# Matmuls of ones ahead of two score matmuls at the start of layer 1's cross-attention

## The chip, the core and the metric

The kernel runs on one core of one Trainium2 chip. A core has five engines with a queue each: TensorE (in the profile PE for the matmuls and PEld for the loading of their weights), VectorE (DVE), ScalarE (ACT), GpSimd (POOL) and SyncE (SP, which here only issues DMAs). Matmuls write to PSUM, which has eight banks of 2 KB per partition. The metric is the device time of one execution in microseconds, the median of several runs. The profile is of one execution, taken apart from these runs.

## The reference

A decoder of two layers works on x, 16 sequences of 256 tokens with 128 channels, and on a context of 16 x 64 rows. Everything is float32. Each layer adds a self-attention, a cross-attention and a feed-forward part with experts to x. The change lies where layer 1's self-attention ends and its cross-attention begins:

```python
def _L1_xattn_ref(x, latents, w_q, w_kv, w_out, b_out):   # 16 heads of 8 channels
    q = latents @ w_q.T                                   # latents: the normed x
    k, v = jnp.split(x @ w_kv.T, 2, axis=-1)              # x here: the context
    ...
    attn = jnp.einsum('blhd,bshd->bhls', q, k) * SCALE
    attn = jax.nn.softmax(attn, axis=-1)
    out = jnp.einsum('bhls,bshd->blhd', attn, v)
    return out.reshape(B, L, DIM) @ w_out.T + b_out

x = x + _L1_attn_ref(_layernorm(x), ...)
x = x + _L1_xattn_ref(ctx_1024, _layernorm(x), ...)   # the context and the latents
x = x + _L1_ffn_ref(_layernorm(x), ...)
```

(In the call as the kernel computes it, queries come from the normed x and keys and values from the context, so every token has 64 scores for each of 16 heads.)

## The kernel before, in words

The kernel works through the layers in phases. Layer 1's self-attention is one phase; cross-attention and the feed-forward part of layer 1 are the next one, and the last. Each phase opens pools of PSUM banks of its own on the banks that the phase before has given back. Self-attention has four banks of scores, three small ones (a pool of tag `m`, L1584) and one of outputs. The last phase has one tile `sx` of four banks, two small banks (again a tag `m`, in the pool `ps_m` of that phase) and two for the feed-forward part. `misc` (L1511) takes the next of the small banks.

Within the phase, x is cut into 8 chunks of 512 tokens, and a chunk into 4 row tiles of 128 tokens. A part is a small function that issues one step for one row tile, one pair of tiles (a sequence) or one chunk. The order of the parts is written out by hand: a word such as `S2:0` means part S2 for chunk 0, and every engine executes its own instructions in the order in which the words issue them. There is a list of words for the start, one plan that repeats for the chunks, and one list for the end. Self-attention's order is written out in the same way. Where the phases meet, an engine's instructions of the new phase can lie between the last ones of the old phase.

The parts for row tile i that matter here, in the order in which a tile goes through them:

- `S` (L1979, its matmul L1983) multiplies the keys of the tile's sequence with its queries: four float32 matmuls, one for each group of 32 partitions, into one half of `sx`. Tiles 0, 2, ... take the one half, tiles 1, 3, ... the other. A float32 matmul is two pieces in the profile.
- `G` (L1990, VectorE) finds the greatest score per head, negated; `B` (L1994, VectorE) subtracts it, reading `sx` for the last time and writing `px` in SBUF; `E` (L2002, ScalarE) is the exponential.
- `A` (L2008 and L2009, GpSimd) adds halves of the 64 probabilities; `R` (L2016 and L2017, VectorE) finishes the sum and takes the reciprocal; `Q` (L2022, GpSimd) spreads it.
- `T` with a half of the heads (`flip`, L2039, its matmul L2043) transposes four blocks of 128 x 128 probabilities into a small bank `tx`; `C` (L2052, ScalarE) copies that bank to SBUF as `pTx`.
- `V` (L2061) multiplies with the values, and so on to the output of the cross-attention.

The start of the phase is these words: S1 and S0, then G0, G1 and B0 on VectorE, S2 (which overwrites tile 0's half of `sx`, so it waits for B0), G2, E0, T01 (tile 0, second half of the heads), B1 and B2, E1, S3 (which in the trace starts when B2 has ended), C01 and so on. S0 and S1 of chunk 1 follow, whose maximum is `G0:1`.

The last steps of self-attention that matter here are the product `y` with the output weights (L1712, TensorE, into one of the three small banks) and its addition to x (L1716, VectorE).

At the very start of the whole kernel stand 18 matmuls of ones by ones (L1048), 36 pieces in the profile. The tile `ones` (L107) is 128 x 128 in SBUF and never changes.

Of the kernel before, what the change touches and what calls it, by code (L numbers as in the profile page):

```python
# [22 lines left out]
P = 128  # L23
# [5 lines left out]
TPC = CH // P  # L29
# [19 lines left out]
W = D + 2  # L49
# [18 lines left out]
def kernel(ctx: ExitStack, tc: tile.TileContext, a: dict, out: bass.AP):  # L68
    nc = tc.nc
# [37 lines left out]
    ones = const.tile([P, P], F32, tag="ones", name="ones")  # L107
# [140 lines left out]
    with ExitStack() as ph:  # L248
# [229 lines left out]
        PARTS = ((0, slice(0, P)), (1, slice(P, 3 * P)))  # L478
# [39 lines left out]
        def flip(u):  # L518
            b, pair = u
            halves = tp_of[u] = [  # L520
                ps_m.tile([P, 2, 3, HP], F32, tag="m", name=f"t0_{b}_{pair}_{r}") for r in range(2)
            ]
            for i in range(2):
                pr = pr_of.pop((b, 2 * pair + i))
                for blk in range(3):
                    for r in range(2):
                        rows = slice(r * HP, (r + 1) * HP)
                        nc.tensor.transpose(  # L528
                            halves[r][:, i, blk, :], pr[rows, blk * P : (blk + 1) * P],
                            ident[rows, rows],  # L530
                        )

        def flipped(u, r):
            b, pair = u
            if r == 0:
                pT_of[u] = pp.tile([P, 2, 3, 2, HP], F32, tag="pT", name=f"pT0_{b}_{pair}", bufs=3)
            nc.vector.tensor_copy(pT_of[u][:, :, :, r, :], tp_of[u][r])  # L537
# [500 lines left out]
        with tc.manual_schedule(engines=ordered | {mybir.EngineType.Pool}):  # L1038
# [104 lines left out]
            for i in range(steps // 2):  # L1143
# [4 lines left out]
                def unit(k, j, *rest):  # L1148
                    if not 0 <= j < n:
                        return  # L1150
                    u = units[j]
                    {
                        "S": scores, "T": flip, "V": values, "G": greatest, "E": exponentials,
                        "R": reciprocal, "N": scaled, "C": flipped, "O": values_out,
                    }[k](u, *rest)

                for tok, lag in plan_of:
                    k = tok[0]
# [157 lines left out]
    with ExitStack() as ph:  # L1316
# [87 lines left out]
        def down(i):  # L1404
            s = state[i]
            ps = s["y"] = ps_m.tile([P, D], F32, tag="m", name=f"y0_{i}")
            for f in range(NF0):
                nc.tensor.matmul(  # L1408
                    ps, s["hT"][:, f, :],
                    dn0[:, bass.ds(s["e"], 1), f, :].rearrange("p e d -> p (e d)"),  # L1410
                    start=(f == 0), stop=(f == NF0 - 1),
                )
# [96 lines left out]
    held = {}  # L1509

    def misc(key, shape):  # L1511
        held[key] = room["m"].tile(shape, F32, tag="m", name="_".join(map(str, key)))
        return held[key]
# [11 lines left out]
    def part_root(what, c):  # L1525
        mv = held["mv", what, c]
        ve = lnp.tile([P, TPC], F32, tag="ve", name=f"ve_{what}_{c}")
        nc.gpsimd.tensor_scalar(ve, mv[:, :, 1], LN_EPS, None, ALU.add)
        rstd = lnp.tile([P, TPC], F32, tag=f"rstd_{what}", name=f"rstd_{what}_{c}")
        nc.gpsimd.tensor_tensor(rstd, ve, nhalf, ALU.pow)  # L1530
        held["rstd", what, c] = rstd
        if what == "f":
            nb = held["nb", c] = lnp.tile([P, TPC], F32, tag="nb", name=f"nb_{c}")
            nc.gpsimd.tensor_tensor(nb, mv[:, :, 0], rstd, ALU.mult)
            nc.gpsimd.tensor_scalar(nb, nb, -1.0, None, ALU.mult)
# [429 lines left out]
    with ExitStack() as ph:  # L1965
# [69 lines left out]
        def shares_out(b):  # L2035
            held["rT", b] = xp.tile([P, N], F32, tag="rT", name=f"rT_{b}")
            nc.scalar.copy(held["rT", b], held.pop(("rt", b)))

        def flip(u, half):  # L2039
            ps = misc(("tx", u, half), [P, 4, P])  # L2040
            for m in range(4):
                h = 8 * half + 2 * m
                nc.tensor.transpose(  # L2043
                    ps[:, m, :],
                    held["pr", u][:, h : h + 2, :].rearrange("p h j -> p (h j)"), ident,
                )
# [178 lines left out]
        def added(c, t):  # L2225
            if ("yo", c) not in held:
                held["yo", c] = hbp.tile([P, TPC, D], F32, tag="yo", name=f"yo_{c}")
            yo = held["yo", c]
            nc.vector.tensor_tensor(
                yo[:, t, :], x[c][:, t, :],  # L2230
                bank(t) if c == NCHUNK - 1 else held.pop(("yf", c, t)), ALU.add,
            )
            held["made", c, t] = True
            if ("made", c, t ^ 1) in held:
                t -= t % 2
                r0 = c * CH + t * P
                nc.sync.dma_start(
                    out_rows[r0 : r0 + 2 * P, :].rearrange("(t p) d -> p t d", p=P),
                    yo[:, t : t + 2, :],
                )  # L2240

        PARTS = {"xt": xt, "xc": xc, "xb": xb, "xq": xq, "xQ": xQ, "xr": lambda c: part_root("x", c)}
# [10 lines left out]
        for i in range(TPC):  # L2253
            for key, what in (
                ("S", scores), ("G", greatest), ("B", below), ("E", exponential), ("R", sums),
                ("A", quarters), ("Q", shares_of),
            ):
                PARTS[f"{key}{i}"] = lambda c, i=i, what=what: what(TPC * c + i)
            for half in range(2):
                PARTS[f"T{i}{half}"] = lambda c, i=i, half=half: flip(TPC * c + i, half)  # L2260
                PARTS[f"C{i}{half}"] = lambda c, i=i, half=half: flipped(
                    TPC * c + i, half, nc.scalar.copy
                )
                PARTS[f"D{i}{half}"] = lambda c, i=i, half=half: flipped(
                    TPC * c + i, half, nc.vector.tensor_copy
                )
            PARTS[f"d{i}"] = lambda c, i=i: down(c, i)
            PARTS[f"z{i}"] = lambda c, i=i: added(c, i)
# [21 lines left out]
        plan = [part.split(":") for part in PLAN.split()]  # L2290
        with tc.manual_schedule(engines=ordered | {mybir.EngineType.Pool}):
            for word in (
                "xs1:2 S1:0 S0:0 G0:0 G1:0 B0:0 S2:0 G2:0 E0:0 T01:0 B1:0 B2:0 E1:0 S3:0"
                " C01:0 A1:0 E2:0 G3:0 T11:0 A0:0 T21:0 T10:0 B3:0 C11:0 R1:0 Q1:0 S0:1 S1:1"
                " C21:0 R0:0 T00:0 E3:0 T30:0 C10:0 G0:1 A2:0 T20:0 C00:0 C30:0 Q0:0 C20:0"
                " G1:1 A3:0 K0:2 P0:0 V0:0 B1:1 B0:1 R3:0 U0:0 T31:0 S2:1 E0:1 O0:0 Q3:0"
                " C31:0 xt:2 Y0:0 R2:0 G2:1 Q2:0 E1:1 X0:0 B2:1 xc:2 P1:0 U1:0 A0:1 E2:1"
            ).split():
                part, c = word.split(":")
                PARTS[part](int(c))  # L2300
            for c0 in range(1, 7):
                for part, lag in plan:
                    if 0 <= c0 - int(lag) < NCHUNK and (part, c0 - int(lag)) not in begun:
                        PARTS[part](c0 - int(lag))
            for word in (
                "xb:7 fs0:6 R0:7 V1:6 A1:7 O1:6 S3:7 a1:5 z1:4 A2:7 T21:7 m1:5 Y1:6 C21:7"
                " X1:6 fs1:6 h2:5 a2:5 T10:7 fr:6 m2:5 h3:5 C10:7 a3:5 T11:7 R1:7 C11:7 m3:5"
                " T01:7 C01:7 fn:6 G3:7 Q0:7 T00:7 T20:7 D20:7 k2:5 C00:7 Q1:7 h4:5 k3:5"
                " k1:5 pk:7 B3:7 a4:5 P0:7 ft:6 m4:5 U0:7 R2:7 j4:5 fc:6 V0:7 fl:6 O0:7 h0:6"
                " Y0:7 a0:6 d3:5 d0:5 E3:7 Q2:7 fg:6 fe:6 T30:7 A3:7 T31:7 C30:7 X0:7 m0:6"  # L2310
                " z3:5 z0:5 fs0:7 C31:7 fq:6 d2:5 fw:6 R3:7 h1:6 Q3:7 fW:6 a1:6 z2:5 P1:7"
                " U1:7 V1:7 O1:7 Y1:7 m1:6 X1:7 h2:6 a2:6 fs1:7 m2:6 h3:6 a3:6 m3:6 j3:6"
                " h4:6 fr:7 fn:7 ft:7 a4:6 m4:6 fc:7 d1:5 z1:5 fl:7 j2:6 k4:6 h0:7 k1:6 a0:7"
                " fg:7 d3:6 m0:7 fe:7 z3:6 d0:6 fq:7 h1:7 fw:7 a1:7 fW:7 m1:7 h2:7 i1:7 a2:7"
                " z0:6 d2:6 m2:7 h3:7 j1:7 a3:7 e0:7 d1:6 m3:7 j3:7 h4:7 e1:7 i2:7 z2:6 a4:7"
                " m4:7 j2:7 e3:7 z1:6 k4:7 e4:7 e2:7 z3:7 z2:7 z1:7 z0:7"
            ).split():
                part, c = word.split(":")
                PARTS[part](int(c))
# [59 lines left out]
```

## Time and profile before

| | us |
|---|---|
| median of three runs | 1401.31 (1401.13 to 1402.62) |
| the profiled execution | 1399.55 |
| its span, first to last instruction | 1397.8 |

| stretch of the span, us | PE busy | DVE busy | ACT busy | POOL busy | granted clock |
|---|---|---|---|---|---|
| 0 to 830 | 800.62 | 616.96 | 485.04 | 473.44 | 1.00 |
| 830 to 1149 (self-attention of layer 1) | 305.29 | 296.08 | 304.70 | 124.76 | 0.99 |
| 1149 to 1180 (where the phases meet) | 23.61 | 19.36 | 14.59 | 9.50 | 0.78 |
| 1180 to 1398 | 206.36 | 173.23 | 138.30 | 135.13 | 1.00 |

All times are microseconds from the first instruction. The page cuts the span into 40 equal slices and gives each engine's busy share as a digit in tenths, and in the line PEclk the granted clock of TensorE in tenths of full speed. The same can be asked for any stretch. In the timeline a row is the start, the time it took, the engine, the line, the operation, what it writes and reads, its shape and how many pieces are merged; in brackets stands how long the engine was idle before, and what released it. The chain that ended last is followed back from the last instruction: each step is what released the step after it, or what stood before it on its engine. A matmul's end is modelled, and the pieces of one row overlap.

### The profile page before, as it was taken

How to read it: one execution, taken by the hardware profiler on the slowest of the kernel's cores; microseconds unless marked ns; L12 is line 12 of the kernel's file. 1: busy time of each engine (PE TensorE's matmuls, PEld its weight loads, DVE VectorE, ACT ScalarE, POOL GpSimd, SP SyncE). 2: the span in 40 equal slices, each digit the busy share in tenths (PEclk: the TensorE clock that was granted, in tenths of full speed). 3: DMA queues.
4: the chain of work that ended last, by engine and by line, in shares of the span. 5: the costliest groups of instructions: out<-in, count | busy, mean ns of one | idle time of the engine just before them, and what ended most of it. 6: DMA issues, size and time to landing. Idle time of an engine off the chain costs nothing.

```text
span 1397.8 us, 38026 instructions
## 1 busy us (share of the span) xinstructions
PE 1335.9 (96%) x13209; PEld 997.3 (71%) x13209; DVE 1105.6 (79%) x4481; ACT 942.6 (67%) x2533; POOL 742.8 (53%) x1226
## 2 busy tenths in 40 slices
PE   9999999999999999799899989999999987899998
PEld 7777777777777777689899966666666654566665
DVE  5776877777777768677679769999999977988874
ACT  6776666767675766354233349999999984776663
POOL 6463748575666656745533373543344314667751
PEclk9999999999999999999999999999999998999999
DMA  6773000000000000467667520000000000113112
GB/s 163 235 241 90 2 5 10 10 7 11 7 10 9 17 9 19 152 201 239 198 225 233 172 71 24 17 15 12 17 2 3 3 2 1 31 43 73 39 43 65
DMA packets 80085, 95.33 MB, mean 68 GB/s; under 512 B 19564, under 2 KB 62828, under 8 KB 79896
## 3 DMA queue, kind: packets, MB, share of 16 engines
q1 hardware_dynamic: 65064, 45.72, 11.9%
q10 hardware_dynamic: 10512, 38.28, 8.1%
q0 software_dynamic: 4320, 8.92, 1.9%
q8 instruction: 106, 1.74, 0.5%
q14 instruction: 83, 0.68, 0.2%
HBM read 63.72 MB, written 29.16 MB: 66 GB/s over the span
## 4 chain that ended last, share of the span: by engine, by line
PE 67%; ACT 17%; DVE 12%; issue 2%; POOL 1%; another core or an unknown queue 1%; DMA 0%; ACTq 0%; DVEq 0%; POOLq 0%
ACT p L1752 8%; PE pqk L418 8%; PE o L550 5%; PE s L473 5%; PE y L450 4%; PE g L1390 4%; PE t L528 4%; PE u L1390 4%; PE y L1408 4%; PE pv L435 3%; PE t L1770 3%; PE g L2173 2%; ACT pT L1781 2%; PE s L1730 2%; PE o L1794 2%; PE u L2173 2%
## 5 line engine op out<-in xcount | busy, mean ns | idle before, releaser
L512 POOL TENSOR_SCALAR p<-p,rs 128x128 f32<-128x128 f32 (+1 forms) x512 | 213.3, 431 | 166.1 <-DVE rs L506 124.3
L498 ACT ACTIVATE p<-p,nm 128x128 f32<-128x128 f32 (+1 forms) x512 | 226.4, 446 | 24.5 <-DVE nm L486 20.1
L1752 ACT ACTIVATE p<-p,nm 128x256 f32<-128x256 f32 x512 | 220.9, 508 | 1.7 <-DVE nm L1741 0.4
L1741 DVE CUSTOM_DVE_ANT_0 p<-s,strip 128x256 f32<-128x256 f32 x512 | 186.7, 419 | 14.7 <-PE s L1730 13.8
L537 DVE COPY pT<-t 128x384 f32<-128x384 f32 x256 | 130.2, 550 | 38.9 <-PE t L528 37.5
L486 DVE CUSTOM_DVE_ANT_0 p<-s,strip 128x128 f32<-128x128 f32 (+1 forms) x512 | 154.2, 348 | 0.5 <-PE s L473 0.2
L1419 POOL DMA_INDIRECT rows_out<-yr,to x71 | 68.8, 969 | 116.3 <-DVE yr L1417 110.6
L1770 PEld LDWEIGHTS t<-ident,p 64*128 64x128 f32 x2048 | 79.7, 139 | 54.4 <-ACT pT L1781 15.3
L550 PEld LDWEIGHTS o<-pT,v 128*64 128x64 f32 x1024 | 64.2, 138 | 66.4 <-issue 34.1
L429 ACT ACTIVATE k<-pqk 128x512 f32<-128x512 f32 x64 | 38.1, 596 | 108.3 <-PE pqk L418 108.3
L1770 PE MATMUL t<-ident,p 64*128 64x64 f32 x2048 | 102.4, 231 | 8.1 <-ACT pT L1781 2.7
L1398 ACT ACTIVATE gs<-gs 128x512 f32<-128x512 f32 x71 | 44.7, 630 | 85.3 <-DVE gs L1397 73.5
L473 PE MATMUL s<-k,q 64*128 64x128 f32 (+1 forms) x1024 | 100.4, 332 | 0.3 <-DVE nm L486 0.3
L550 PE MATMUL o<-pT,v 128*64 128x256 f32 (+1 forms) x1024 | 99.0, 335 | 0.6 <-DVE pT L537 0.6
L498 ACT ACTIVATION_READ_ACCUMULATOR p<-p,nm 128x1 f32 x512 | 97.9, 191 | 0.0
L528 PE MATMUL t<-ident,p 64*128 64x64 f32 x1536 | 81.2, 228 | 14.2 <-ACT pre L742 4.7
L528 PEld LDWEIGHTS t<-ident,p 64*128 64x128 f32 x1536 | 68.3, 138 | 35.8 <-POOL p L512 9.0
L1730 PE MATMUL s<-k,q 32*128 32x256 f32 x1024 | 86.3, 409 | 1.4 <-DVE nm L1741 1.4
L1781 ACT COPY pT<-t 128x512 f32<-128x512 f32 x144 | 81.1, 588 | 5.1 <-PE t L1770 4.3
L444 DVE COPY v<-pv 128x512 f32<-128x512 f32 x64 | 44.2, 691 | 50.5 <-PE o L550 28.0
L1390 PE MATMUL g<-xTs,gu 128*128 128x128 f32 x568 | 76.9, 279 | 3.6 <-ACT xTs L1362 3.5
L1390 PE MATMUL u<-xTs,gu 128*128 128x128 f32 x568 | 76.8, 276 | 3.3 <-issue 3.3
(375 smaller groups left out, 3356.1 us busy)
## 6 DMA issues: line engine op xcount, KB each, us to landing
gu<-in_L_ffn_gate_up_w ACTq DMA_DIRECT2D x71, 512.0 KB
rows_in<-zero SPq DMA_DIRECT2D x131, 130.0 KB
spread<-wrows SPq DMA_DIRECT2D x14, 512.0 KB
xr<-rows_in SPq DMA_DIRECT2D x71, 65.0 KB
y<-rows_out SPq DMA_DIRECT2D x16, 256.0 KB
out_x<-yo SPq DMA_DIRECT2D x16, 128.0 KB
x<-in_x SPq DMA_DIRECT2D x7, 256.0 KB
rows_out<-yr,to POOLq DMA_INDIRECT x71
```

The costliest lines, as they stand in the source:

```text
L473: nc.tensor.matmul(ps_of[b, h][:, cols], q[rows, u2, iq], k[rows, u2, 0:nk], start=True, stop=True,)
L486: nc.vector.tensor_tensor_reduce(out=pr[:, cols], in0=ps[:, cols], in1=strip[:, h, P : 2 * P] if it == 0 else strip[:, h, :], scale=1.0, s ...
L498: nc.scalar.activation(pr[:, cols], pr[:, cols], AF.Exp, bias=nm[:, it : it + 1], scale=-1.0, accum_out=sm[:, it : it + 1],)
L512: nc.gpsimd.tensor_scalar(pr[:, cols], pr[:, cols], rs[:, it : it + 1], 1.0, ALU.mult, ALU.mult)
L528: nc.tensor.transpose(halves[r][:, i, blk, :], pr[rows, blk * P : (blk + 1) * P], ident[rows, rows],)
L537: nc.vector.tensor_copy(pT_of[u][:, :, :, r, :], tp_of[u][r])
L550: nc.tensor.matmul(po[rows, c0:N], v[:, jt, h % 8 * DH : (h % 8 + 1) * DH], pT[:, 0:N] if jt == 0 else pT[:, N:], start=(jt == 0), stop=(j ...
L1390: nc.tensor.matmul(ps[:, f, :], gu[:, lo + f * P : lo + (f + 1) * P], xT, start=True, stop=True,)
L1730: nc.tensor.matmul(ps_of[b, h][:, it, :], q[rows, it * P : (it + 1) * P], k[rows, s4, :], start=True, stop=True,)
L1741: nc.vector.tensor_tensor_reduce(out=pr[:, it, :], in0=ps[:, it, :], in1=strip1[:, h, (1 - it) * P : (1 - it) * P + N], scale=1.0, scalar= ...
L1752: nc.scalar.activation(pr[:, it, :], pr[:, it, :], AF.Exp, bias=nm[:, it : it + 1], scale=-1.0)
L1770: nc.tensor.transpose(halves[r][:, k, jt, it, :], pr[rows, it, jt * P : (jt + 1) * P], ident[rows, rows],)
```

## The change

A new part `W` with a row tile and a half takes the small bank that the same tile's `T` will write, and issues 14 matmuls of `ones` by `ones` into its four quarters in turn, each starting and ending its own sum. `T` then uses the bank that `W` took, if there is one, and its transposes overwrite what the ones left. Two words are added to the list of the start: `W01:0` between B0 and S2 (the bank of T01), and `W11:0` between E1 and S3 (the bank of T11). On TensorE they stand directly ahead of the third and the fourth tile's scores. Nothing else is changed, and no result depends on the added products.

```diff
+        def keep(u, half, times):
+
+            ps = misc(("tx", u, half), [P, 4, P])
+            for k in range(times):
+                nc.tensor.matmul(ps[:, k % 4, :], ones, ones, start=True, stop=True)
+
         def flip(u, half):
-            ps = misc(("tx", u, half), [P, 4, P])
+            ps = held.get(("tx", u, half)) or misc(("tx", u, half), [P, 4, P])
...
             for half in range(2):
+                PARTS[f"W{i}{half}"] = lambda c, i=i, half=half: keep(TPC * c + i, half, 14)
...
-                "xs1:2 S1:0 S0:0 G0:0 G1:0 B0:0 S2:0 G2:0 E0:0 T01:0 B1:0 B2:0 E1:0 S3:0"
+                "xs1:2 S1:0 S0:0 G0:0 G1:0 B0:0 W01:0 S2:0 G2:0 E0:0 T01:0 B1:0 B2:0 E1:0 W11:0 S3:0"
                 " C01:0 A1:0 E2:0 G3:0 T11:0 A0:0 T21:0 T10:0 B3:0 C11:0 R1:0 Q1:0 S0:1 S1:1"
```

## The prediction

> **What bounds the kernel now.** I read the page's slices first. TensorE is busy nearly everywhere, and of the slices ahead of the last two, the one around 1170 us is the emptiest in the kernel and the only one whose granted clock shows less than 9.
>
> ```profile
> span 1397.8 us, 38026 instructions
> PE   9999999999999999799899989999999987899998
> PEclk9999999999999999999999999999999998999999
> ```
>
> One slice is 34.9 us; the 8 is the 34th, 1153 to 1188 us. There layer 1's self-attention ends and its cross-attention begins, and the change sits in it. Next I read that stretch in the timeline of TensorE (start, length, line, what it writes, count, idle time before and its releaser):
>
> ```profile
> 1159.32 0.71 PE L1712 MATMUL y<-wo,oT 128*128 128x128 f32 x4
> 1163.30 1.24 PE L1983 MATMUL sx<-kb,qx 32*128 32x256 f32 x8 [3.27 <-DVE px L1994]
> 1164.57 1.11 PE L2043 MATMUL tx<-ident,px 128*128 128x128 f32 x4
> 1168.15 1.24 PE L1983 MATMUL sx<-kb,qx 32*128 32x256 f32 x8 [2.47 <-DVE px L1994]
> 1169.32 2.91 PE L2043 MATMUL tx<-ident,px 128*128 128x128 f32 x12
> 1172.16 2.09 PE L1983 MATMUL sx<-kb,qx 32*128 32x256 f32 x16
> ```
>
> TensorE ends self-attention's last product y at 1160.03 and idles 3.27 us until S2, the third tile's scores, may overwrite the first tile's half of sx; before S3 it idles 2.47 us again. VectorE is the releaser both times. The third view is busy time per stretch; the columns are length, then PE, PEld, DVE, ACT, POOL, then the granted clock.
>
> ```profile
> 1157.34:1160.75 3.41, 2.69 (x12) 1.38 (x10) 1.62 (x4) 0.37 (x1) 0.00 (x0) 1.00 0.03 5
> 1160.75:1164.16 3.41, 0.86 (x8) 0.52 (x8) 2.50 (x3) 0.80 (x1) 0.00 (x0) 0.50 0.00 0
> 1164.16:1167.58 3.42, 1.50 (x8) 0.71 (x4) 2.97 (x3) 0.93 (x2) 0.00 (x0) 0.50 0.00 0
> 1167.58:1170.99 3.41, 2.84 (x16) 2.08 (x16) 2.02 (x3) 2.61 (x4) 2.69 (x3) 0.50 0.00 0
> 1170.99:1174.40 3.41, 3.41 (x23) 2.17 (x22) 2.15 (x6) 2.27 (x4) 2.98 (x5) 0.50 0.00 0
> ```
>
> The clock is half from 1160.75 to 1174.40, exactly four steps of 3.41 us. The other falls (566.83, 699.95, 843.31) last one step each, and all lie on the same 3.413-us grid. So this execution decides the clock at fixed moments, by what the step just ended held. S2 and S3 take 1.24 us here and 0.71 us at 1184.64, where the clock is full.
>
> The fourth view is the chain that ended last.
>
> ```profile
> 1168.15 1.24 PE sx L1983 x8
> 1169.39 2.84 PE tx L2043 x12
> 1172.23 2.06 PE sx L1983 x16
> 1174.29 0.02 issue
> 1174.31 2.37 DVE nmx L1990 x2
> ```
>
> It runs through TensorE at half speed to 1174.29, where the fifth tile's scores release VectorE. After that VectorE leads (9.3 of 10 us busy from 1180 to 1190), then TensorE (119.1 of 120 from 1220 to 1340), so what 1174.31 gains or loses should reach the end. I call that moment **G0:1**. At full clock those pieces, with S2 and the transposes before, would take about half: (1.28 + 0.9 + 1.24 + 2.84 + 2.06)/2 = 4.2 us. That is the most there is to win.
>
> **The change, part by part.** W01 stands behind S0 and y, ahead of S2. W11 stands behind the second tile's exponential and the first tile's transposes (T01), ahead of S3. Each is 14 products of ones, 128x128x128 in float32. L1048 shows the price: 18 products are 36 pieces, so 14 are 28. Read one by one in the timeline, its pieces start 0.213 us apart until 7.03 and 0.112 us apart afterwards (the clock record begins at 7.04). So 28 pieces cost 28 x 0.112 = 3.1 us at full clock and 6.0 us at half. Nothing is removed and no DMA is added; SP and POOL's queues are not passed.
>
> *When W01 may start.* Its bank is the first of a pool that opens where self-attention's pools close, so I take it that the first write waits for the last reader of all of self-attention's small banks. That is L1716, which adds y to x, behind the first maximum on VectorE:
>
> ```profile
> 1160.57 0.41 DVE L1716 TENSOR_TENSOR x<-x,y 128x256 f32<-128x256 f32 x1
> 1160.90 1.22 DVE L1990 TENSOR_REDUCE nmx<-sx 128x16 f32<-128x1024 f32 x1
> 1162.03 1.22 DVE L1994 TENSOR_TENSOR px<-sx,nmx 128x1024 f32<-128x1024 f32 x1
> ```
>
> 0.04 us of signal after 1160.98 gives 1161.02. Before the change nobody saw this wait: the first writer of these banks stood behind S2, which waits for the later L1994. Behind W01 on TensorE stand S2 and everything else; VectorE waits for S2 in G2 and then for nothing until S3.
>
> *Whether the clock is up.* For every grid step I summed the pieces' streaming time, weighted by the share of the array's rows and columns they use. The five steps ahead of a fall hold 0.4 to 1.13 us; every other step at full clock holds 1.26 or more. The step to 1160.75 holds 0.89, and W01 at 1161.02 adds nothing to it, so **the clock falls as before**. In steps at half clock the clock stayed down at 2.47 or less and rose at 2.86 or more. W01 fills 1164.16 - 1161.02 = 3.14 us of the next one, so I let it rise at 1164.16, ten us earlier than now.
>
> [...] Here the record falls 0.72 us after the last piece. [...]
>
> *Sum.* W01 runs 14.7 pieces by 1164.16; the other 13.3 take 1.5 us, to 1165.65. S2, ready at 1163.27, starts there and ends 0.7 later: G2 moves from 1164.61 to 1166.35, **+1.74**. The two subtractions behind it, B1 and B2 (1.14 us each), move as much; B2 ends at 1169.85. W11 starts after T01 (about 1166.8) and ends at 1169.9, under G2, B1 and B2: it costs nothing, and would cost what exceeds 3.1 us if that cover were shorter. S3 then takes 0.7 for 1.24, so G3 is 1.2 late. The 12 transposes and 16 score pieces in front of G0:1 need 1.3 + 1.07 us at full clock, and end near 1173.5. They are no longer last. **What is late next** is POOL: its half sums (L2008, L2009) start at 1168.22 behind the second exponential, which sits behind B1, and take 2.05 + 2.1 us for two tiles; moved by 1.74 they end at 1174.1. VectorE reads them (0.41 and 0.25 us, L2016, L2017) ahead of G0:1: 1174.75 for 1174.31, **+0.45**, say +0.5. The profiled execution would go from 1399.55 (span 1397.8 and 1.75 around it) to 1400.05. The three timed runs' median, 1401.31, lies 1.76 above that execution; the same half us gives **1401.8**.
>
> Another execution may have its grid elsewhere. Worked through with the same weights for all positions, the forecast's kind of fall (somewhere between 1158.9 and 1161.5) gives +0.4 to +2.1, since before the change too the clock comes back earlier at some of them.
>
> **Rivals.**
> - **A, the clock holds.** For: W01 shortens the idle time to 1.0 us, and for grid positions with boundaries from 1161.6 on it is already in the deciding step. Then W01 ends at 1164.15, G2 is 0.24 late, POOL's sums end at 1172.6, G0:1 comes at 1173.3: **-1.0** (1400.3), -0.2 where the old clock recovered sooner. Against: the profiled step of 0.89.
> - **B, W01's bank is free at once.** Its own bank was last read by L1693, which ends at 1157.7. W01 then starts at 1160.03, puts 0.72 us into the deciding step (1.61, no fall), ends at 1163.16 and hides wholly: G2 at 1164.0 (-0.6), POOL's sums 1171.75, G0:1 at 1172.4: **-1.9** (1399.4). Against: the pool's boundary.
> - **C, slower: the ones do not bring the clock back in time.** Place: W01 ahead of S2. If 3.14 of 3.41 us is not enough, all 28 pieces run at half: S2 starts at 1167.0, G2 at 1168.2 (+3.55), G0:1 by POOL at 1176.6: **+2.3** (1403.6). Should the clock still be down when W11 runs, S3 waits 6.0 us for it and comes at 1175.1 for 1168.15: +7 (1408). It decides from a rise later than 1167.6. For: 2.84 busy us did not suffice at 1170.99. Against: L1048 itself rises after its first filled step.
> - **D, the whole cold stretch is repaid** and POOL is not late: -4.2 (1397.1). Against: W01 alone is longer than the 2.28 us between 1161.02 and S2.
>
> **How the numbers follow.** Forecast 0.45, A 0.25, B 0.08, C 0.15 (a third of it the +7), D 0.07. Over 0.2%, 2.8 us and about what a measurement of this kernel can tell from no change, lie D on one side, and on the other the +7 and about half of the rest of C and the ends of the forecast: faster 0.07, within 0.81, slower 0.12. The range takes in A, B and the lesser C with a few tenths for the spread of the runs (1401.13 to 1402.62), 1399.2 to 1403.8; D, the +7 and some of C, 0.17, stay out.
>
> **What would show it.** Right: W01's first piece starts within 0.1 us of the end of L1716; the clock is half for one step only; its pieces change from 0.213 to 0.112 apart on the way; S2 starts near 1165.6, S3 near 1169.9 without idle time caused by W11; the fifth tile's maximum waits for L2017 and no longer for sx. Wrong: W01 next to y (B), clock 1.00 throughout (A), S2 at 1167 (C), or a later step that now falls because work has shifted against the grid: the step 1198.29 to 1201.71 holds only 1.28, and one more fall would cost up to 1.7.

## The result, and the profile after

| | before | after |
|---|---|---|
| median over the runs compared, us | 1400.91 (18 runs) | 1403.58 (18 runs) |
| ratio, 95% interval | | 1.0021 [1.0013, 1.003] |
| the profiled execution, us | 1399.55 | 1405.24 |

The change costs 0.21%, 2.9 us (1.8 to 4.2 by the interval). The forecast was 0.5 us. The page of the changed kernel, where code lines behind the insertion stand 6 lower than before:

```profile
span 1403.5 us, 38138 instructions
PE   9999999999999999799899989999999988899998
PEclk9999999999999999999999999999999999999999
```

The 112 added instructions are 56 matmul pieces and 56 weight loads. The 8 has become a 9 in PEclk: the cold stretch is gone from the page, and yet the kernel is slower.

Two executions of one kernel can't be laid over each other from their starts, because the part ahead of the change differs from one to the next: the last y (L1712) starts between 1156.97 and 1166.29 us in the executions below. So I cut each trace at two events. **Lead** is the stretch from the start of that y to the start of the ninth maximum on VectorE (L1990). **Rest** is the stretch from there to the end of the span; some expectations call it the tail. Before: lead 31.59, rest 206.93. After: lead 32.32, rest 208.78. So the change loses **0.73 us in the lead** and **1.85 us in the rest**, 2.58 together, within the interval of the runs.

**The lead.** The timeline of TensorE after the change (start, length, line, what it writes, count, idle before and its releaser):

```profile
1162.40 0.71 PE L1712 MATMUL y<-wo,oT 128*128 128x128 f32 x4
1164.12 4.93 PE L2043 MATMUL tx<-ones 128*128 128x128 f32 x28 [1.00 <-DVE x L1716]
1168.98 0.71 PE L1983 MATMUL sx<-kb,qx 32*128 32x256 f32 x8
...
1170.12 3.29 PE L2043 MATMUL tx<-ones 128*128 128x128 f32 x28
1173.34 0.71 PE L1983 MATMUL sx<-kb,qx 32*128 32x256 f32 x8
```

W01 waits for L1716 on VectorE and then takes 4.93 us. S2 has no idle time ahead of it any more: it starts 6.58 us behind y's start, where it started at 3.98 before. The 3.29 us of W11, at a granted clock of 1.00, are full speed for the same 28 pieces. Busy time by clock step (length, PE, PEld, DVE, ACT, POOL, then the granted clock):

```profile
1160.56:1163.97 3.41, 2.56 (x11) 1.38 (x10) 1.66 (x3) 0.37 (x1) 0.00 (x0) 1.00 0.02 5
1163.97:1167.38 3.41, 3.26 (x15) 3.26 (x16) 2.36 (x3) 0.93 (x1) 0.00 (x0) 0.50 0.00 0
1167.38:1170.80 3.42, 3.42 (x34) 2.97 (x34) 1.03 (x1) 0.21 (x1) 0.00 (x0) 1.00 0.00 0
```

One step at half clock instead of four, and it is the step that W01 fills. VectorE shows what ends late in its place:

```profile
1169.77 1.23 DVE L1990 TENSOR_REDUCE nmx<-sx 128x16 f32<-128x1024 f32 x1 [3.43 <-PE sx L1983]
...
1177.57 0.42 DVE L2016 TENSOR_REDUCE smx<-half 128x16 f32<-128x256 f32 x1 [0.35 <-POOL half L2009]
1178.03 0.25 DVE L2017 RECIPROCAL smx<-smx 128x16 f32<-128x16 f32 x1
1178.20 2.29 DVE L1990 TENSOR_REDUCE nmx<-sx 128x16 f32<-128x1024 f32 x2
```

VectorE idles 3.43 us for S2, and the fifth tile's maximum (1178.20) stands behind POOL's half sums and no longer waits for scores.

**The rest.** Between the ninth maximum and some 170 us later both kernels keep step to 0.05 us. Then the chain of the changed kernel shows two DMAs that the chain of before does not have:

```profile
1365.26 3.34 DMA wrows<-cTf
1368.66 0.58 SPq L2163
1369.29 6.73 DMA spread<-wrows
```

They belong to the experts of the last chunk but one: `fW` (L2145 of before) writes 8 rows of routing weights, 16 KB, to memory and reads them back spread over 128 partitions, so the second DMA's issue waits for the first to land (1368.60, the issue at 1368.66). In the queue of SyncE before:

```profile
1361.49 0.30 SPq L2152 DMA_DIRECT2D wrows<-cTf  x1
1363.01 1.24 SPq L2157 DMA_DIRECT2D spread<-wrows  x2
```

1.52 us lie between the issues; after the change 3.40 (1365.26 to 1368.66). VectorE, which multiplies by `spread`, pays for it:

```profile
1376.15 0.69 DVE L2195 TENSOR_TENSOR hb<-hb,spread 128x512 f32<-128x512 f32 x1 [2.71 <-DMA spread<-wrows]
```

Before, this wait was 0.81 us:

```profile
1370.47 0.69 DVE L2189 TENSOR_TENSOR hb<-hb,spread 128x512 f32<-128x512 f32 x1 [0.81 <-DMA spread<-wrows]
```

TensorE's next yf then waits 1.51 us for POOL's share of the same product, and from there the chain is TensorE's until 1399.45.

Why is one small write late, 200 us behind the change? The DMA queues of the changed kernel from 1365.2 to 1368.7 (packets, MB, share of the DMA engines' time) show a stranger at that moment, one 16 KB packet on the queue that the page calls `q8 instruction`:

```profile
q1 hardware_dynamic: 288, 0.15, 15.3%
q8 instruction: 1, 0.02, 2.7%
```

Before, from 1361.4 to 1363.1, there are the 288 packets of q1 alone. The times of single packets are from the trace's packet records. Over the kernel this queue has 106 such packets before and 107 after, one for about 250 instructions of TensorE (26,418 and 26,530). That they carry TensorE's code is read from this count and from the runs below, where added TensorE instructions move them; the records name no engine. The stranger starts 170.98 us behind the ninth maximum and lasts 1.49 us; the write is issued at 170.54, and its last packet, landed at 171.69 before, lands at 173.29. Before the change no packet of that queue lies between 161.2 and 182.3.

### The profile page after: what moved, and what is told of

Its sections match the earlier page's. It is cut to its first block, busy times and chain, and to the rows that moved or that the text cites. A ratio compares the mean times of both kernels' runs of the same rounds, so it can differ in the third digit from the quotient of the medians.

```text
span 1403.5 us, 38138 instructions
## 1 busy us (share of the span) xinstructions
PE 1341.1 (96%) x13265; PEld 1002.5 (71%) x13265; DVE 1106.1 (79%) x4481; ACT 943.4 (67%) x2533; POOL 742.9 (53%) x1226
## 4 chain that ended last, share of the span: by engine, by line
PE 68%; ACT 16%; DVE 10%; POOL 2%; issue 2%; DMA 2%; another core or an unknown queue 1%; SPq 0%; DVEq 0%; ACTq 0%; POOLq 0%
ACT p L1752 8%; PE pqk L418 8%; PE o L550 5%; PE s L473 5%; PE g L1390 4%; PE y L450 4%; PE u L1390 4%; PE y L1408 4%; PE t L528 4%; PE pv L435 3%; PE t L1770 3%; PE o L1794 2%; PE s L1730 2%; ACT pT L1781 2%; PE g L2179 2%
```

## Experiments

Theory 1: W01 is longer than the wait it fills, and that is the whole cost; the late DMA is the chance of one execution. Theory 2: the late DMA belongs to the change, too. With e1 to e4 this became more definite: **added TensorE instructions move the moment at which TensorE's next 16 KB of code arrives, here onto a small write that the end waits for.** Theory 3: W11 is what costs.

All runs together, before the single ones; "code packet" is the start of the packet of q8 nearest to the write, behind the ninth maximum:

| kernel | TensorE instructions added | lead | rest | code packet | ratio to before, 95% |
|---|---|---|---|---|---|
| before | 0 | 31.59 | 206.93 | 161.2, 182.3 | |
| after | 112 | 32.32 | 208.78 | 170.98 | 1.0021 [1.0013, 1.003] |
| e1_again | 112 | 32.37 | 208.83 | 171.85 | 1.0018 [1.0006, 1.003] |
| e2_w01_only | 56 | 32.38 | 206.89 | 178.0 | 1.0009 [0.9998, 1.0021] |
| e3_w11_only | 56 | 31.78 | 206.90 | 178.1 | 1.001 [0.9999, 1.0021] |
| e4_tile_wait | 112 | 30.16 | 208.44 | 171.43 | 0.9998 [0.9987, 1.001] |
| e5_tile_14_6 | 80 | 29.72 | 209.04 | 171.54 | 0.9985 [0.9972, 0.9998] |
| e6_eight | 64 | 31.60 | 206.93 | 178.2 | 0.9995 [0.9984, 1.0005] |
| e7_start_46 | 112, elsewhere | 31.59 | 208.36 | 171.07 | one execution |
| e8_after_start_32 | 168 | 32.38 | 206.89 | 167.6 | one execution |
| e9_tile_10_6 | 64 | 29.70 | 206.93 | 177.9 | 0.9991 [0.998, 1.0001] |
| e10_tile_14_2 | 64 | 29.83 | 206.93 | 178.2 | 0.9995 [0.9983, 1.0007] |
| e11_tile_14_6_again | 80 | 29.70 | 206.96 | 171.70 | one execution |
| e12_tile_only | 0 | 31.59 | 206.97 | 161.0, 182.1 | one execution |

**e1_again** is the changed kernel once more, with no edit.

> The changed kernel once more, for a second profile of it. I measure the lead: start of the ninth maximum (L1990, from which on the two kernels ran in step to 0.02 us) less the start of self-attention's last product y (L1712). Before 1190.9 - 1159.3 = 31.6, after 32.3, so the change cost 0.7 there; 1.9 more were lost near 1370, where the profile after waits for a DMA of the spread weights. Theory 1 (W01 is longer than the wait it fills, and by where the clock's steps fall it costs 0 to 2 us there; the DMA is chance): lead between 31.4 and 33.7, the wait near 1370 need not come again, ratio about 1.001 to 1.003. Theory 2 (the later DMA wait belongs to the change): it comes again, the stretch from the ninth maximum to the end is again near 208.8 against 206.9.

Lead 32.37 and rest 208.83, each within 0.05 of the first profile. The late DMA is no chance of one execution: theory 1 falls in that half. (The expectation's "in step to 0.02 us" is 0.05 when every instruction of the two traces up to the late write is compared.)

**e2_w01_only** leaves W11 out:

```diff
-                "xs1:2 S1:0 S0:0 G0:0 G1:0 B0:0 W01:0 S2:0 G2:0 E0:0 T01:0 B1:0 B2:0 E1:0 W11:0 S3:0"
+                "xs1:2 S1:0 S0:0 G0:0 G1:0 B0:0 W01:0 S2:0 G2:0 E0:0 T01:0 B1:0 B2:0 E1:0 S3:0"
```

> W11 taken out, W01 left. Theory 1 (all of the loss is W01 in front of S2): lead as after, 32.3 or a little less, S2 2 to 3 us behind where it was, S3 within 0.1 of the changed kernel's; ratio 1.001 to 1.003. Theory 3 (W11, in front of S3, is what costs): lead at or below 31.6, ratio 1.000 or less.

The whole loss of the lead is there (32.38), none of the loss of the rest (206.89). Without W11 the clock falls a second time, for one step 11.5 us behind y, and the lead doesn't notice.

**e3_w11_only** leaves W01 out:

```diff
-                "xs1:2 S1:0 S0:0 G0:0 G1:0 B0:0 W01:0 S2:0 G2:0 E0:0 T01:0 B1:0 B2:0 E1:0 W11:0 S3:0"
+                "xs1:2 S1:0 S0:0 G0:0 G1:0 B0:0 S2:0 G2:0 E0:0 T01:0 B1:0 B2:0 E1:0 W11:0 S3:0"
```

> W01 taken out, W11 left. Theory 1: S2 as before; the clock falls as before; W11 starts after T01, runs at half until the clock's next step and ends about 1.5 us after S3 could start, but S3 and what follows run at full clock; POOL is not late, since the second exponential is not; lead 31.4 to 31.8, ratio 0.9995 to 1.0005. Theory 3 (W11 costs): lead 32.3 or more.

W11 alone costs the lead 0.19 and the rest nothing; theory 3 falls. Neither half of the change shows the loss of the rest, and the whole does. That speaks against any cause that lies in one of the parts, and for one that counts instructions.

**e4_tile_wait** keeps both parts and takes away what W01 waits for. The pool of the small banks tracks its reuse tile by tile, so that W01 waits for what last used its own bank and no longer for L1716:

```diff
-        ps_m = ph.enter_context(tc.tile_pool(name="ps_ml1", bufs=2, space=PSUM))
+        ps_m = ph.enter_context(tc.tile_pool(name="ps_ml1", bufs=2, space=PSUM, reuse_waits="tile"))
```

> The changed kernel with one word more: the pool of the small banks lets a tile wait for the last reader of its own bank instead of for all of self-attention's small banks. W01 then need not wait for L1716. Theory 1: W01 starts when y's last piece has been issued, about 1 us earlier against y; it lies wholly in TensorE's idle time if the clock holds, S2 waits for L1994 again, lead 29.7 to 30.5 with the clock up throughout, ratio 0.998 to 0.999. If the clock falls all the same, W01 is at half for a part and the lead is 31 to 32.5, ratio 1.000 to 1.001. Rival (the wait does not matter): ratio as after.

```profile
1164.09 0.71 PE L1712 MATMUL y<-wo,oT 128*128 128x128 f32 x4
1164.64 3.29 PE L2043 MATMUL tx<-ones 128*128 128x128 f32 x28
1168.07 0.71 PE L1983 MATMUL sx<-kb,qx 32*128 32x256 f32 x8
1169.33 0.66 PE L2049 MATMUL tx<-ident,px 128*128 128x128 f32 x4 [0.55 <-ACT px L2002]
1169.83 3.29 PE L2043 MATMUL tx<-ones 128*128 128x128 f32 x28
```

W01 follows y at once and takes 3.29 us, all at full clock, and S2 starts 3.98 behind y as before. The clock does not fall near here (W01 and W11 take 3.29 us each, S2 and S3 0.71, as at a granted clock of 1.00), and the lead is 1.43 shorter than before. So the wait for L1716 was the cost of W01. Now W11 has less cover: S3 comes 4.97 behind S2 here, against 4.36 in the changed kernel. The rest is long again (208.44): 112 instructions, and the packet at 171.43. So the ratio misses the 0.998 to 0.999 that I had expected: the rest takes back what the lead gains.

**e5_tile_14_6** is e4 with a shorter W11:

```diff
-                PARTS[f"W{i}{half}"] = lambda c, i=i, half=half: keep(TPC * c + i, half, 14)
+                PARTS[f"W{i}{half}"] = lambda c, i=i, half=half: keep(TPC * c + i, half, 14 if i == 0 else 6)
```

> W01 keeps its 14 products and waits only for the last readers of its own bank, as in e4; W11 has 6 products in place of 14, so TensorE has 80 instructions more than before instead of 112. Theory 2 (the later loss is a collision of TensorE's own code fetch, a 16 KB packet, with the small wrows write, and its place is set by the number of instructions ahead): the fetch moves to about 175 us after the ninth maximum, between its places with 56 more (178.0) and 112 more (171.0), and misses the write at 170.6 to 172: stretch up to the ninth maximum 30.0 to 30.4 (31.59 before), rest 206.9, about 1.4 us under before, ratio near 0.999. Theory 1 (the later DMA wait is chance, or belongs to the reuse of banks): rest about 208.4 as in e4, ratio 1.000.

The lead fell to 29.72, 0.28 below the least I had expected: with 6 products S3 stands 4.32 behind S2, so W11 is free again. For the rest theory 2's number was wrong: 80 instructions put the packet at 171.54, not at the 175 that I had drawn between its places at 56 and 112, and the rest was 209.04. The packet's place is no straight line of the count: 56 and 64 instructions give 177.9 to 178.2, 80 and 112 give 171.0 to 171.9, and nothing was seen between. Why it keeps to these two places was not tried. And the runs don't fit the profile: lead and rest of the profile say +0.24 us against before, the ratio says -2.1 (-3.9 to -0.3). e11 takes this up.

**e6_eight** is the change with 8 products for 14 in both parts, still waiting for L1716:

```diff
-                PARTS[f"W{i}{half}"] = lambda c, i=i, half=half: keep(TPC * c + i, half, 14)
+                PARTS[f"W{i}{half}"] = lambda c, i=i, half=half: keep(TPC * c + i, half, 8)
```

> W01 and W11 have 8 products each in place of 14, and W01 waits for L1716 as in the change. W01 starts 1.7 us after y; the clock falls as before and holds half for one step or two. If the first loss is W01's length beyond the wait it fills, W01's 16 pieces end 1.3 us earlier than the 28 or so, G2 comes about 1.3 earlier than the change's 7.36, and the ninth maximum between 30.9 and 31.6 (32.32 with the change, 31.59 before). If one step with few products no longer brings the clock back, the ninth maximum comes at 32 or later. Theory 2: 64 instructions more than before, the fetch near 177, rest 206.9. Theory 1: rest 208 or more in this one too.

W01's pieces start from 1.71 to 4.91 behind y (28 pieces: to 6.37), S2 at 5.11 for 6.58, and the maximum G2 at 5.89 for 7.36. The clock comes back after one step and falls again for another 11.5 us behind y; lead 31.60, as before. Rest 206.93, as theory 2 had it, with the packet at 178.2 (177 expected). A shorter W01 loses nothing and wins nothing.

**e7_start_46** is the kernel before with 112 more TensorE instructions at the very start of the kernel, some 1150 us ahead of the place of the change:

```diff
-            for _ in range(18):
+            for _ in range(46):
                 nc.tensor.matmul(first_ps[0][:, 0, :], ones, ones, start=True, stop=True)
```

> The kernel before, without W01 and W11, and with 28 more products of ones at the kernel's start (46 in place of 18): as many TensorE instructions as the change adds, 112, in another place. The start is some 6 us longer. Theory 2: the stretch up to the ninth maximum as before (31.6), and the rest 208.5 to 208.9 with a code packet at about 171 after the ninth maximum, though nothing has been changed in layer 1. Theory 1 or any theory that puts the later loss on the work in cross-attention: rest 206.9.

The lead is that of before to 0.01 us, and the rest 208.36, with the packet at 171.07. In SyncE's queue 2.95 us lie between the issues, where they were 1.52:

```profile
1368.44 0.30 SPq L2152 DMA_DIRECT2D wrows<-cTf  x1
1371.39 1.24 SPq L2157 DMA_DIRECT2D spread<-wrows  x2
```

Nothing of layer 1 was touched. The loss of the rest needs neither W01 nor W11, nor any added work near them. (Expected: 208.5 to 208.9; 208.36 is a little under that.)

**e8_after_start_32** is the changed kernel with 14 more products at the start, 168 instructions more than before:

```diff
-            for _ in range(18):
+            for _ in range(32):
                 nc.tensor.matmul(first_ps[0][:, 0, :], ones, ones, start=True, stop=True)
```

> The changed kernel with 14 more products of ones at the kernel's start (32 in place of 18): 168 TensorE instructions more than before in all. Theory 2: the code packet leaves 170.6 to 172, as it did with every other count; the stretch up to the ninth maximum stays at 32.3 and the rest falls back to 206.9. Any theory that puts the later loss on the two added parts: rest 208.8.

*More* work removes the second loss: packet at 167.6, rest 206.89, while the lead keeps its first loss (32.38). With e7 this is the sharpest pair, though each is one execution: the loss of the rest is put in without the change, and taken out with it.

**e9_tile_10_6** has 10 products in W01 and 6 in W11, with tile waits, 64 instructions. Against e5:

```diff
-                PARTS[f"W{i}{half}"] = lambda c, i=i, half=half: keep(TPC * c + i, half, 14 if i == 0 else 6)
+                PARTS[f"W{i}{half}"] = lambda c, i=i, half=half: keep(TPC * c + i, half, 10 if i == 0 else 6)
```

> W01 waits for its own bank alone and has 10 products, W11 has 6: 64 TensorE instructions more than before, as many as in the run with 8 and 8, whose code packet lay at 178.2 after the ninth maximum, clear of the wrows write. Theory 2 (the later loss is decided by the count of added instructions alone): rest 206.9, stretch up to the ninth maximum 29.7 to 30.4 if 10 products still keep the clock up, so 1.2 to 1.9 us under before and a ratio of 0.9987 to 0.9991. If the later loss belonged to the banks' reuse (both runs with it so far had it), the rest is 208.4 to 209.1.

Lead 29.70, rest 206.93: 1.89 us less than before by its profile, and the clock full from y to the ninth maximum (1.00 in every step from 1157.70 to 1171.34, y starting at 1159.78). The ratio, 0.9991 [0.998, 1.0001], agrees with -1.9 us but does not exclude zero. Against the changed kernel (1.0021 [1.0013, 1.003]) the two intervals lie apart.

**e10_tile_14_2** has 14 and 2, again 64 instructions. Against e5:

```diff
-                PARTS[f"W{i}{half}"] = lambda c, i=i, half=half: keep(TPC * c + i, half, 14 if i == 0 else 6)
+                PARTS[f"W{i}{half}"] = lambda c, i=i, half=half: keep(TPC * c + i, half, 14 if i == 0 else 2)
```

> As the run before, with 14 products in W01 and 2 in W11: again 64 instructions more, and again rest 206.9 by theory 2. If W11's products are not needed to keep the clock up, the stretch up to the ninth maximum is 29.5 to 29.9; if the step behind W01 is too empty without them, the clock falls for a step and the stretch is 30.5 to 31.6.

Rest 206.93 as expected. The clock falls for one step 8.75 us behind y, where it stayed up with 6 products; that costs 0.13 of lead, less than expected. By its profile this kernel takes 1.76 us less than before; its ratio, 0.9995 [0.9983, 1.0007], shows less, and its interval takes in both that and no change.

**e11_tile_14_6_again** is e5 word for word.

> The kernel with 14 and 6 products, word for word: its one profile had the late wrows write (rest 209.0), while its median over the runs was 1.9 us under before, 2.1 us better than that profile. If the collision is in every execution, rest 208.5 to 209.1 again; if it comes and goes with the execution, rest 206.9 is possible, with a code packet outside 170.5 to 172.5. Stretch up to the ninth maximum 29.7 either way.

The loss comes and goes, but not by the way I had set down. The packet is where it was, at 171.70 (e5: 171.54), and yet the rest is 206.96. The write's last packet has landed at 171.67, 0.03 us ahead of the code; in e5 it landed at 173.18, behind it. The two executions in SyncE's queue, e5 first:

```profile
1361.97 0.30 SPq L2158 DMA_DIRECT2D wrows<-cTf  x1
1365.60 0.58 SPq L2163 DMA_DIRECT2D spread<-wrows  x1
```

and e11:

```profile
1361.04 0.30 SPq L2158 DMA_DIRECT2D wrows<-cTf  x1
1362.55 1.24 SPq L2163 DMA_DIRECT2D spread<-wrows  x2
```

One program, 3.63 and 1.51 us between the issues. So e5's median can be better than its one profile. How many of the timed runs had the collision can't be read without their profiles.

**e12_tile_only** is before with the edit of e4's pool and no products:

```diff
-        ps_m = ph.enter_context(tc.tile_pool(name="ps_ml1", bufs=2, space=PSUM))
+        ps_m = ph.enter_context(tc.tile_pool(name="ps_ml1", bufs=2, space=PSUM, reuse_waits="tile"))
```

> The kernel before with the small banks' waits taken tile by tile and nothing else: no products. Without an early first write nobody waits for the banks, so stretch 31.6 and rest 206.9, as before. A stretch under 31 would say that the gain of the runs with tile waits is not that of the products.

Lead 31.59, rest 206.97: the tile wait alone is worth nothing. The gain of e9 is that of products that may start early.

## Why the prediction was wrong

Step by step, as the prediction put them, with its times turned into distances from y's start:

- *W01 waits for L1716.* Right: its first piece starts 0.05 us behind the end of L1716. e4 shows the wait's price. It is rival B made true, with the clock up throughout, and its lead changes by -1.43 where B had -1.9: B had no term for W11, which then has less cover. With 6 products in W11 it is -1.87 (e5) and -1.89 (e9).
- *The clock falls as before and rises after one step.* Right: it falls 1.57 us behind y's start (before 1.43), for one step. Rivals A and C fall with it. TensorE had ended y 0.9 us before the fall, the whole gap up to W01 was 1.00 us, and the step ahead of the fall had been busy for 2.56 of its 3.41 us.
- *W01 ends at 6.33, G2 +1.74.* S2 started at 6.58 and G2 was +2.08. The mechanism is right and the size 0.34 short: 0.25 of it ahead of S2, the rest between S2 and its maximum.
- *W11 is hidden.* Right within 0.04 (e2 without it: S3 4.32 behind S2; with it 4.36). e4 shows what the prediction called the shorter cover: 0.65.
- *POOL is late next.* Right, and later by the same third of a microsecond: its first half sum starts at 10.98 for 8.90, the fifth tile's maximum comes at +0.80 instead of +0.45, and 0.73 are left at the ninth.
- *"Nothing is removed and no DMA is added", and what 1174.31 loses should reach the end.* **This is the step that failed.** The 0.73 did reach the end. But 112 instructions are code, and the traces show code coming in by DMA: the page's queue `q8 instruction` had 107 packets for 106, and one of them started 170.98 us behind the ninth maximum (in the kernel before, none between 161.2 and 182.3). The sum counts the instructions' time on TensorE and not their bytes; it has no term for them. In the profile that term was 1.85 us, 2.5 times the other one. e7 and e8 tie it to how many instructions are added ahead of the write, and not to where they stand; e5 and e11 show one program with the loss and without it, 0.16 us apart in the packet's start (171.54 and 171.70).

The median, 1403.58, lies inside the stated range and next to rival C's 1403.6, and both are chance: C had S2 7.7 us behind y and the ones at half clock throughout, where S2 came at 6.58 and the clock was back after one step, and no part of the range was there for a late write.

The prediction had named "a later step that now falls because work has shifted against the grid" as what could go wrong. No such step took part: the clock record of the changed kernel is full from 1167.39 to 1402.91. The code packets are 16 KB each, one for about 250 TensorE instructions. TensorE shows no wait for the one near the write: from 1364.46 to 1380.51 its timeline marks only two idle times, 0.67 us ended by VectorE and 1.51 us ended by POOL. The write that the packet met came later: its last packet landed 173.29 us behind the ninth maximum, before the change 171.69.

What stays open is how the code packet delays the write. In all five executions with the loss (after, e1, e4, e5, e7) it overlaps the write in time, and in none without it. In each of the five, seven of the write's eight packets land by 171.67 as before, and one alone is late: it starts as the code packet ends (within 0.01 us in e1, e4 and e5) or 0.7 us after that (after and e7, where the code packet starts 0.3 us ahead of the write's first). That both share one DMA engine would explain it, but the packets' engines are not in the records, so it is not shown. e3's ratio, 1.001, is higher than its profile's +0.16 us explains; its interval takes in both.

## What to carry to other kernels

Here 112 instructions added to TensorE, even where they cost the lead nothing (e7: 31.59, as before), shifted a later code packet (171.07; in the kernel before, none between 161.2 and 182.3) and cost the rest 1.43 us: list the small DMAs that the end waits for, see in the packets of before how near the code queue's packets lie, and try the same number of instructions at another place before a loss is blamed on the edit. Filler that keeps TensorE's clock up was worth what its first wait allowed (lead +0.73 with the wait for L1716, -1.43 without it in e4, -1.89 in e9): see what its bank waits for before its length is chosen. And cut two traces at common events; the sum of one stretch's loss and another's was visible only so.

## What was not expected of the hardware

- A 16 KB write of 8 packets, on its way for 1.1 us, landed up to 1.6 us later where a 16 KB code packet of 0.9 to 1.5 us overlapped it; its last packet came 0.2 to 0.8 us behind the end of the code packet in all five executions. The end of the kernel moved by 1.4 to 2.1 us.
- 0.16 us in the start of that packet separate, in one program, an execution with the loss from one without it (171.54 and 171.70).
- The clock of TensorE fell to half with only 0.6 to 1.1 us of idle time behind y in every execution in which nothing followed y for 1.0 us or more, and never near here in e4, e5, e9 and e11, where products followed y at once and 6 or more stood in W11.
